# A selective-scan hybrid block: decays written into the state's tile, the scalar engine three states ahead, transfers issued one planner step later, and one row fetch per state in place of two

## The chip, the cores and the metric

The kernel runs on one core of one Trainium2 chip. A core has a matrix engine (PE, whose weight loads the profile shows as PEld), a vector engine (DVE), a scalar engine (ACT), GpSimd (POOL) and SyncE (SP), which here only issues transfers. Each engine works through its own list of instructions in order, and an instruction waits at the head of its list until the semaphores that it names have been reached. Transfers are carried out by 16 DMA engines that the core's queues share. The metric is the device time in microseconds (us) of the whole launch; a kernel's time is the median of its runs.

## The reference, cut to what matters

The input is a batch of 8 images of 64 x 64 pixels and 96 channels, in float32. Layer 0 is a group norm, an in-projection to 2 x 192 channels, a 3 x 3 depthwise convolution with SiLU, a selective scan along four directions (diagonals and anti-diagonals, each forward and backward), a layer norm, a gate and an out-projection. Layer 1 is a linear attention without softmax and a feed-forward part whose operands are rounded to 8-bit floats. The scan dominates the work:

```python
def step(hst, inp):
    u_t, d_t, B_t, C_t = inp
    hst = hst * jnp.exp(d_t[..., None] * A) + (d_t * u_t)[..., None] * B_t[:, :, None, :]
    return (hst, jnp.einsum('bkdn,bkn->bkd', hst, C_t))
h0 = jnp.zeros((Bsz, K, D_INNER, D_STATE), jnp.float32)
_, yL = jax.lax.scan(step, h0, (uL, dL, BL, CL))
ys = jnp.moveaxis(yL, 0, -1) + Dk[None, :, :, None] * xs
```

There are K = 4 directions, 192 inner channels, D_STATE = 16 states for each channel, and 4096 positions in an image. Each state is a recurrence of its own: a decay exp(d A), a feed (d u) B, the running value h, and a product with C that is summed over the 16 states.

## The kernel before

**Tiling.** Positions lie along the free dimension, 512 at a time (T). The partitions hold 64 channels of two directions at once (d = 0 and 1), and G = 3 groups make up the 192 channels; so one state of one chunk is a tile of 128 x 3 x 512. The order of chunks is `steps`: for each of 8 images (b), two passes (q = 0 forward, q = 1 backward) over 8 chunks (c), 128 steps in all. Each step goes through its 16 states, so that the main loop (L1155) has 2048 iterations, one state each. In what follows i is the iteration, m the step and n the state in it.

**One state.** ACT computes the decay (`decay`, L961): three ACTIVATEs with Exp, one for each group, into a tile of the tag "decay" with three buffers. The feed comes in one of three ways, by the letter of `FEED = "DADADAGADADAAAAA"` (L48). In an A state ACT multiplies the turned rows of d u with B (`times_b`, L968, L988), eight ACTIVATEs into feedT (two buffers), and PE turns these back into the three PSUM tiles feed[0..2] (`turn`, L996). In the one G state POOL does ACT's eight products (L979). In a D state PE broadcasts B into feed[0] (L998) and DVE multiplies it with d u (L1013). Then DVE runs the recurrence with one scan instruction for each group (`recur`, L1000, scan at L1009), from the decay tile and the feed into an h tile, which has six buffers. POOL keeps the last column for the next chunk (`keep`, L1025) and multiplies h in place with C (`read`, L1030). C comes as the tile cc of 128 x 512, whose two halves hold one row each, repeated over 64 partitions: `fetch` (L952) reads the two rows from a DRAM tile crow, with two transfers (L957); cc has five buffers. Last, PE adds the products up by transposing them into one PSUM tile y (`reduce`, L1032, L1044).

**The order of an iteration.** Iteration i issues the decay of state i + 2, some background work for ACT, `times_b` of i + 2, the scans of i, then for three parts the turn of i + 1 and the reduce of i - 4 (`LAG = 4`) with background work for PE between, the keep and read of i - 1, background work for POOL, and the fetch of i + 4. The program text sets each engine's order; the tile framework adds the waits. A tile of a tag with N buffers waits for the last users of the tile N before it.

**Background work.** All that is not a state is written as Python generators and spread by a planner, `Work` (L261): `measures` and `front` (norm, convolution, gate, and the walk along the diagonals) for the next image, `tail` (join, attention, feed-forward) for the image before, and `prologue` (L879), which makes d, d u, B and C of the step after next. A generator yields a request: an engine, a cost in us, perhaps a lag, and whether it needs one of two PSUM banks. The planner places it when the engine's credit for the iteration allows (`PLACES`) and no earlier than a lag that depends on the two engines (`LAGS`; after a transfer, three iterations). The requests of tag "S", for SP, are looked at when an iteration begins (`next`, L337). Where there is no scan work to lean on, `finish` and `hurry` run the background alone.

**Transfers.** All transfers are issued from SP's one queue, in program order: also a transfer whose data are not made yet waits at the head of that queue, and what was issued later waits behind it. In this kernel a transfer stands right behind the instruction that makes its data: gate at L561, seq at L599, mid at L689, turned at L728, out at L834, crow at L910, part at L1072 (an image's first pass) and wide at L1089 (the second). The table gives the sizes.

Of the kernel before, what the change touches and what calls it, by code (L numbers as in the profile page):

```python
# [255 lines left out]


SPIN = ("P", 0.0, -1, False)


class Work:  # L261
# [104 lines left out]
    def finish(self, enough):  # L366

        self.alone = True
        while not enough():
            self.next()  # L370
            for tag, place in (("A", 0), ("V", 0), ("P", 2), ("G", 0)):
                self.at(tag, place)
        self.alone = False
        self.credit = dict.fromkeys(self.PLACES, 0.0)

    def hurry(self, enough):

        self.alone = self.hurried = True
        while not enough():
            self.now += 1  # L380
            for tag, place in (("A", 0), ("V", 0), ("P", 2), ("G", 0)):
                self.at(tag, place)
        self.alone = self.hurried = False
# [90 lines left out]
def front(tc, work, x, k, at, b):  # L474
# [8 lines left out]
    with tc.tile_pool(name=f"f1_{b}", bufs=1, **area) as p1, tc.tile_pool(name=f"f2_{b}", bufs=2, **area) as p2:  # L483
# [33 lines left out]
        def convolve(c):  # L517
# [41 lines left out]
            nc.scalar.activation(z, z, AF.Silu)  # L559
            k.tables()  # L560
            nc.sync.dma_start(out=at.gate[:, :, c * CH : (c + 1) * CH], in_=z)  # L561

# [13 lines left out]
    with tc.tile_pool(name=f"f3_{b}", bufs=3, **area) as p2:  # L576

        def walk(c):
# [12 lines left out]
            for g in range(G):  # L591
# [4 lines left out]
                nc.scalar.copy(u[:, g, :], ps)  # L596
                work.release(ps)
            for d in range(2):
                nc.sync.dma_start(  # L599
                    out=at.seq[d][:, c * T : (c + 1) * T].rearrange("(g i) t -> i g t", i=GC),  # L600
                    in_=u[d * GC : (d + 1) * GC],
                )
# [5 lines left out]
def tail(tc, work, x, out, k, at, b, last=False):  # L608
# [4 lines left out]
    with tc.tile_pool(name=f"t1_{b}", bufs=1, **area) as p1:  # L613
# [5 lines left out]
        with tc.tile_pool(name=f"t2_{b}", bufs=8 if last else 2, **area) as p2:  # L619
# [3 lines left out]
            def join(c):  # L623
# [63 lines left out]
                nc.scalar.copy(t, po)  # L687
                if not last:
                    nc.sync.dma_start(out=at.mid[:, s, :], in_=t)  # L689
                work.release(ps)  # L690
# [34 lines left out]
                if last:  # L725
                    kept[c] = t, xaT
                else:
                    nc.sync.dma_start(out=at.turned[:, c * CH : (c + 1) * CH], in_=xaT)  # L728
                joined.add(c)
# [32 lines left out]
        with tc.tile_pool(name=f"t3_{b}", bufs=8 if last else 3, **area) as p2:  # L762

            def layers(c):
# [67 lines left out]
                nc.gpsimd.tensor_tensor(y16, y16, k.b2q, ALU.add)  # L832
                nc.gpsimd.tensor_tensor(t, t, y16, ALU.add)
                nc.sync.dma_start(out=out[b].rearrange("(t p) c -> p t c", p=P)[:, s, :], in_=t)  # L834

# [3 lines left out]
def run(tc, psum, dram, x, out, w, NB):  # L839
# [33 lines left out]

    made, decays, feeds, hs, carry, sums, other = {}, {}, {}, {}, {}, {}, {}
    feed = [psum.tile([P, T], F32, tag=f"feed{g}", name=f"feed{g}") for g in range(G)]
# [3 lines left out]
    def prologue(m):  # L879
# [27 lines left out]
        nc.scalar.activation(x, v, AF.Identity, bias=w.xb)  # L907
        work.release(ps)
        o.crow = dram.tile([2 * NS, T], F32, tag="crow", name=f"crow_{m}", bufs=3)
        nc.sync.dma_start(out=o.crow, in_=x[XC:NX, :])  # L910
# [3 lines left out]
        for g in range(G):  # L914
            ps = yield bank(0.85)
            nc.tensor.matmul(ps, w.ws[:, q, g, :], x[0 : 2 * NR + 1, :], start=True, stop=True)  # L916
# [35 lines left out]
    def fetch(i):  # L952

        m, n = divmod(i, NS)
        cc = made[m].c[n] = pool.tile([P, T], F32, tag="cc", name=f"cc_{i}", bufs=5)
        for d in range(2):
            nc.sync.dma_start(  # L957
                out=cc[d * GC : (d + 1) * GC], in_=made[m].crow[d * NS + n : d * NS + n + 1, :].to_broadcast([GC, T])
            )

    def decay(i):  # L961
        m, n = divmod(i, NS)
        _, q, _ = steps[m]
        decays[i] = pool.tile([P, G, T], F32, tag="decay", name=f"decay_{i}", bufs=3)
        for g in range(G):
            nc.scalar.activation(decays[i][:, g, :], made[m].delta[:, g, :], AF.Exp, scale=w.a_neg[:, q, g, n : n + 1])  # L966

    def times_b(i):  # L968
# [3 lines left out]
        if FEED[n] == "D":  # L972
            return
        f = feeds[i] = pool.tile([P, TB * G, P], F32, tag="feedT", name=f"feedT_{i}", bufs=2)
        if FEED[n] == "G":
# [24 lines left out]
    def recur(i):  # L1000
        m, n = divmod(i, NS)
        _, q, _ = steps[m]
        h = hs[i] = pool.tile([P, G, T], F32, tag="h", name=f"h_{i}", bufs=6)
        a = decays.pop(i)
        back = slice(None, None, -1) if q else slice(None)

        def scan(g):
            init = carry[m - 1][:, n, g : g + 1] if m % NST else 0.0
            nc.vector.tensor_tensor_scan(h[:, g, back], a[:, g, back], feed[g][:, back], init, ALU.mult, ALU.add)  # L1009

# [47 lines left out]
    def place(m):  # L1058
# [7 lines left out]
        for d in range(2):  # L1066
# [3 lines left out]
            )  # L1070
        if q == 0:
            nc.sync.dma_start(out=image(b).part[:, c, :], in_=ys)  # L1072
        else:
            work.start(spread(m, rows), urgent=True)

    def spread(m, rows):
        b, q, c = steps[m]
        for d in range(2):
            yield gp(1.8, 1)
            nc.gpsimd.tensor_tensor(  # L1080
                rows[:, d], rows[:, d], other[m].rearrange("p (d k c) -> p d k c", d=2, k=TB)[:, d], ALU.add
            )
            stride = (3 * WW + 1) * DI if d == 0 else (3 * WW - 1) * DI
            for v in range(2):
# [59 lines left out]

    LAG = 4
    for i in range(4):
        fetch(i)
    for i in range(2):
        decay(i)
# [5 lines left out]
    for i in range(total + LAG + 1):  # L1155
# [13 lines left out]
        work.next()  # L1169
        if i + 2 < total:  # L1170
            decay(i + 2)
        work.at("A")
        if i + 2 < total:
            times_b(i + 2)
        if i < total:
# [104 lines left out]
```

## Time and profile before

| what | value |
|---|---|
| three runs, us | 11243.42, 11231.5, 11244.23 |
| median, us | 11243.42 |
| the profiled execution's own time, us | 11245.66 |
| its span from first to last instruction, us | 11243.9 |
| granted clock of PE, mean over the span | 0.907 |
| cc transfers | 4096 of 128.0 KB, median issue 588 ns |
| decay ACTIVATE (L966), mean of one | 714 ns |
| feedT ACTIVATE (L988), mean of one | 445 ns |
| scan (L1009), mean of one, with carry / without | 1262 / 1201 ns |
| product with C (L1030), mean of one | 3457 ns |

The profile is of one execution. Busy time is the time in which an engine had an instruction at work; a busy PE is not PE at its peak, since matmuls are pipelined. A line of waits reads: who (engine, tile, line) waited for whom, the total in us, how many times, and the longest. SPq is SP's queue of transfers. The chain is followed back from the last instruction, at each step to what released it, so that it shows what set the end. "DMA share" is the mean busy share of the 16 DMA engines. The first cc transfer is issued at 224.4 us and the last at 10984.2 us: before and after lie the first image's front and the last image's tail.

### The profile page before, as it was taken

To read this page: it belongs to the slowest core of one execution; us is meant where nothing else is said; L and a number is where in the kernel's file an instruction comes from. 1 tells how busy PE (TensorE), PEld (TensorE's weight loads), DVE (VectorE), ACT (ScalarE), POOL (GpSimd) and SP (SyncE) were. 2 spreads that over 40 slices of the span, in tenths; PEclk is the share of its full clock that TensorE was granted. 3 is DMA by queue.
4 is the path that set the end of the run, shared out by engine and by line. 5 is a ranking of instruction groups with operands and counts; after the bars stand their busy time and mean duration, and the time that the engine had idled before them with its cause. 6 is when DMAs were issued, how large, how long until landed. Compare 5 with 4: busy or idle time off the path is not lost.

```text
span 11243.9 us, 182845 instructions
## 1 busy us (share of the span) xinstructions
PE 9140.0 (81%) x60885; PEld 7661.4 (68%) x60885; DVE 9396.9 (84%) x10582; ACT 9455.9 (84%) x19651; POOL 9365.4 (83%) x7047
## 2 busy tenths in 40 slices
PE   6888788878888788878888788887888878878884
PEld 5677677666676667766677666776667666666663
DVE  2988988888888888888888888888898888989993
ACT  3888888888888888888888888888898888888883
POOL 1877987899878998789987899779997799998994
PEclk8999999888998889988999898998999988889886
DMA  3335333543335443354334543345433543432332
GB/s 91 106 92 143 100 98 92 144 118 102 97 93 149 110 108 95 96 144 113 102 92 113 138 107 102 92 118 134 109 99 90 133 119 104 108 103 84 99 94 63
DMA packets 1122742, 1206.98 MB, mean 107 GB/s; under 512 B 452790, under 2 KB 730007, under 8 KB 1121799
## 3 DMA queue, kind: packets, MB, share of 16 engines
q1 hardware_dynamic: 1121798, 1195.28, 40.3%
q8 instruction: 485, 7.95, 0.3%
q14 instruction: 459, 3.75, 0.1%
HBM read 874.83 MB, written 319.98 MB: 106 GB/s over the span
## 4 chain that ended last, share of the span: by engine, by line
PE 24%; ACT 23%; DVE 17%; POOL 14%; issue 10%; DMA 7%; SPq 4%; DVEq 0%; POOLq 0%; ACTq 0%
DVE h L1009 11%; ACT feedT L988 9%; POOL h L1030 8%; ACT decay L966 7%; PE y L1044 7%; PE feed L996 7%; DMA cc<-crow 4%; DVE feed L1013 4%; PE bank L542 3%; SPq L587 2%; PE bank L894 2%; PE feed L998 1%; ACT L63 1%; POOL du L928 1%; DMA y<-wide 1%
## 5 line engine op out<-in xcount | busy, mean ns | idle before, releaser
L1030 POOL TENSOR_TENSOR h<-h,cc 128x1536 f32<-128x1536 f32 x2048 | 7079.9, 3457 | 458.3 <-DMA cc<-crow 228.9
L1009 DVE TENSOR_TENSOR_SCAN h<-decay,carry,feed 128x512 f32<-128x512 f32 x5376 | 6514.2, 1262 | 810.2 <-PE feed L996 704.8
L966 ACT ACTIVATE decay<-delta,a_neg 128x512 f32<-128x512 f32 x6144 | 3975.0, 714 | 1116.4 <-DVE h L1009 1114.4
L996 PE MATMUL feed<-ident,feedT 128*128 128x128 f32 x16896 | 3090.8, 303 | 1649.1 <-DVE h L1009 1084.6
L1044 PE MATMUL y<-ident,h 128*128 128x128 f32 x24576 | 3847.4, 290 | 130.7 <-POOL h L1030 47.4
L996 PEld LDWEIGHTS feed<-ident,feedT 128*128 128x128 f32 x16896 | 2209.1, 155 | 2246.9 <-ACT feedT L988 840.8
L988 ACT ACTIVATE feedT<-duT,rows 128x192 f32<-128x192 f32 x10240 | 3673.7, 445 | 17.6 <-PE feed L996 14.7
L1044 PEld LDWEIGHTS y<-ident,h 128*128 128x128 f32 x24576 | 3164.5, 152 | 525.2 <-issue 410.3
L1013 DVE TENSOR_TENSOR feed<-feed,du 128x512 f32<-128x512 f32 x1920 | 1200.4, 685 | 162.2 <-PE feed L998 146.5
L1025 POOL COPY carry<-h 128x3 f32<-128x3 f32 x2048 | 402.5, 197 | 877.0 <-DVE h L1009 803.2
L1009 DVE TENSOR_TENSOR_SCAN h<-decay,feed 128x512 f32<-128x512 f32 x768 | 879.5, 1201 | 118.9 <-PE feed L996 106.8
L542 PE MATMUL bank<-wf,xp 97*128 97x192 f32 x4266 | 851.9, 332 | 0.0
L998 PE MATMUL feed<-x,pick 77*128 77x512 f32 x1280 | 708.8, 636 | 3.9
L542 PEld LDWEIGHTS bank<-wf,xp 97*128 97x128 f32 x4266 | 692.8, 194 | 5.4 <-issue 4.6
L928 POOL TENSOR_TENSOR du<-delta,u 128x1536 f32<-128x1536 f32 x128 | 448.4, 3503 | 188.8 <-ACT delta L921 188.8
L916 PE MATMUL bank<-x,ws 13*128 13x512 f32 x764 | 435.5, 650 | 5.6 <-ACT x L907 5.6
L979 POOL TENSOR_TENSOR feedT<-duT,rows 128x512 f32<-128x512 f32 x384 | 396.2, 1060 | 4.7 <-PE feed L996 4.7
L894 PE MATMUL bank<-wx,u 128*128 128x77 f32 x3048 | 360.0, 275 | 0.0
L894 PEld LDWEIGHTS bank<-wx,u 128*128 128x128 f32 x3048 | 352.3, 193 | 1.9 <-ACT duT L936 0.2
L918 DVE COPY delta<-bank 128x512 f32<-128x512 f32 x382 | 256.7, 672 | 86.5 <-PE bank L916 86.1
L934 PE MATMUL bank<-ident,du 128*128 128x128 f32 x1532 | 251.8, 291 | 65.1 <-POOL du L928 61.8
L998 PEld LDWEIGHTS feed<-x,pick 77*128 77x128 f32 x1280 | 211.5, 200 | 97.6 <-DVE h L1009 44.8
(261 smaller groups left out, 6957.4 us busy)
## 6 DMA issues: line engine op xcount, KB each, us to landing
cc<-crow SPq DMA_DIRECT2D x4096, 128.0 KB
u<-seq SPq DMA_DIRECT2D x256, 384.0 KB
wide<-ys SPq DMA_DIRECT2D x512, 192.0 KB
ut<-image SPq DMA_DIRECT2D x768, 64.0 KB
seq<-us SPq DMA_DIRECT2D x128, 384.0 KB
part<-ys SPq DMA_DIRECT2D x64, 768.0 KB
y<-part SPq DMA_DIRECT2D x64, 768.0 KB
y<-wide SPq DMA_DIRECT2D x256, 192.0 KB
```

The source lines that it names most:

```text
L542: nc.tensor.matmul(v[:, j, :], flat[:, o : o + P], k.wf[:, i, :], start=(i == 0), stop=(i == 8), skip_group_check=True)
L894: nc.tensor.matmul(v[:, j, :], u[:, g, j * P : (j + 1) * P], w.wx[:, q, g, :], start=(g == 0), stop=(g == G - 1))
L916: nc.tensor.matmul(ps, w.ws[:, q, g, :], x[0 : 2 * NR + 1, :], start=True, stop=True)
L928: nc.gpsimd.tensor_tensor(du, delta, u, ALU.mult)
L966: nc.scalar.activation(decays[i][:, g, :], made[m].delta[:, g, :], AF.Exp, scale=w.a_neg[:, q, g, n : n + 1])
L988: nc.scalar.activation(f[part], o.duT[part], AF.Copy, scale=o.rows[:, j, XB + d * NS + n : XB + d * NS + n + 1])
L996: nc.tensor.transpose(feed[g][:, j * P : (j + 1) * P], feeds[i][:, j * G + g, :], w.ident)
L998: nc.tensor.matmul(feed[0], w.pick[:, FEED[:n].count("D"), :], made[m].x, start=True, stop=True)
L1009: nc.vector.tensor_tensor_scan(h[:, g, back], a[:, g, back], feed[g][:, back], init, ALU.mult, ALU.add)
L1013: nc.vector.tensor_tensor(feed[g], feed[0], made[m].du[:, g, :], ALU.mult)
L1030: nc.gpsimd.tensor_tensor(hs[i], hs[i], c.unsqueeze(1).to_broadcast([P, G, T]), ALU.mult)
L1044: nc.tensor.matmul(y[:, j, :], hs[i][:, g, r * P : (r + 1) * P], w.ident, is_transpose=True, start=(n == 0 and j % 4 == 0), stop=(n == NS ...
```

## The change

Four things are changed.

1. The decay of a state is written into the state's own h tile, and the scan overwrites it in place. The tag "decay" goes, and h has eight buffers in place of six.
2. ACT works three states ahead (`AHEAD = 3`) in place of two, for the decays and for `times_b`; feedT has three buffers in place of two.
3. A new request, `LATER`, of tag "S" and lag 1, stands in front of the transfers of gate, seq, out, crow, part and wide, and of mid and turned together, which are moved to one place. The generator goes on at the start of the next iteration or later, so that the transfer stands that much later in SP's order. The store of part becomes a small generator, `first_rows`. `finish` and `hurry` look at "S" as well. The first bank request in prologue after crow is given a lag of 0.
4. `fetch` reads both rows of a state with one transfer of 128 x 512 in place of two of 64 x 512.

```diff
@@ -255,6 +255,7 @@
     return "P", us, lag, "long" if long else "short"
 
 
+LATER = ("S", 0.0, 1, False)
 SPIN = ("P", 0.0, -1, False)
 
 
@@ -368,7 +369,7 @@
         self.alone = True
         while not enough():
             self.next()
-            for tag, place in (("A", 0), ("V", 0), ("P", 2), ("G", 0)):
+            for tag, place in (("A", 0), ("V", 0), ("P", 2), ("G", 0), ("S", 0)):
                 self.at(tag, place)
         self.alone = False
         self.credit = dict.fromkeys(self.PLACES, 0.0)
@@ -378,7 +379,7 @@
         self.alone = self.hurried = True
         while not enough():
             self.now += 1
-            for tag, place in (("A", 0), ("V", 0), ("P", 2), ("G", 0)):
+            for tag, place in (("S", 0), ("A", 0), ("V", 0), ("P", 2), ("G", 0)):
                 self.at(tag, place)
         self.alone = self.hurried = False
 
@@ -558,6 +559,7 @@
             nc.scalar.activation(pre[:, 0 : len(tiles), :], pre[:, 0 : len(tiles), :], AF.Silu)
             nc.scalar.activation(z, z, AF.Silu)
             k.tables()
+            yield LATER
             nc.sync.dma_start(out=at.gate[:, :, c * CH : (c + 1) * CH], in_=z)
 
             image = at.image[0 : HH * DOUBLE].rearrange("(h a x c) -> h x a c", a=2, c=DI, x=WW)
@@ -595,6 +597,7 @@
                 yield act(0.6)
                 nc.scalar.copy(u[:, g, :], ps)
                 work.release(ps)
+            yield LATER
             for d in range(2):
                 nc.sync.dma_start(
                     out=at.seq[d][:, c * T : (c + 1) * T].rearrange("(g i) t -> i g t", i=GC),
@@ -685,8 +688,6 @@
                         )
                 yield act(0.5)
                 nc.scalar.copy(t, po)
-                if not last:
-                    nc.sync.dma_start(out=at.mid[:, s, :], in_=t)
                 work.release(ps)
                 yield dve(1.7)
                 for i in range(4):
@@ -725,6 +726,8 @@
                 if last:
                     kept[c] = t, xaT
                 else:
+                    yield LATER
+                    nc.sync.dma_start(out=at.mid[:, s, :], in_=t)
                     nc.sync.dma_start(out=at.turned[:, c * CH : (c + 1) * CH], in_=xaT)
                 joined.add(c)
 
@@ -831,6 +834,7 @@
                 yield gp(2.0)
                 nc.gpsimd.tensor_tensor(y16, y16, k.b2q, ALU.add)
                 nc.gpsimd.tensor_tensor(t, t, y16, ALU.add)
+                yield LATER
                 nc.sync.dma_start(out=out[b].rearrange("(t p) c -> p t c", p=P)[:, s, :], in_=t)
 
             yield [layers(c) for c in range(NCH)], 8 if last else 3
@@ -871,7 +875,7 @@
             )
         return images[b]
 
-    made, decays, feeds, hs, carry, sums, other = {}, {}, {}, {}, {}, {}, {}
+    made, feeds, hs, carry, sums, other = {}, {}, {}, {}, {}, {}
     feed = [psum.tile([P, T], F32, tag=f"feed{g}", name=f"feed{g}") for g in range(G)]
     banks = [psum.tile([P, T], F32, tag=f"bank{i}", name=f"bank{i}") for i in range(2)]
     work = Work(banks + feed)
@@ -906,13 +910,14 @@
         x = o.x = tile("x", [NX, T])
         nc.scalar.activation(x, v, AF.Identity, bias=w.xb)
         work.release(ps)
+        yield LATER
         o.crow = dram.tile([2 * NS, T], F32, tag="crow", name=f"crow_{m}", bufs=3)
         nc.sync.dma_start(out=o.crow, in_=x[XC:NX, :])
 
 
         delta = tile("delta", [P, G, T])
         for g in range(G):
-            ps = yield bank(0.85)
+            ps = yield bank(0.85, None if g else 0)
             nc.tensor.matmul(ps, w.ws[:, q, g, :], x[0 : 2 * NR + 1, :], start=True, stop=True)
             yield dve(0.6)
             nc.vector.tensor_copy(delta[:, g, :], ps)
@@ -953,17 +958,17 @@
 
         m, n = divmod(i, NS)
         cc = made[m].c[n] = pool.tile([P, T], F32, tag="cc", name=f"cc_{i}", bufs=5)
-        for d in range(2):
-            nc.sync.dma_start(
-                out=cc[d * GC : (d + 1) * GC], in_=made[m].crow[d * NS + n : d * NS + n + 1, :].to_broadcast([GC, T])
-            )
+        nc.sync.dma_start(
+            out=cc, in_=made[m].crow.rearrange("(d n) t -> d n t", n=NS)[:, n : n + 1, :].to_broadcast([2, GC, T])
+        )
 
     def decay(i):
+
         m, n = divmod(i, NS)
         _, q, _ = steps[m]
-        decays[i] = pool.tile([P, G, T], F32, tag="decay", name=f"decay_{i}", bufs=3)
+        hs[i] = pool.tile([P, G, T], F32, tag="h", name=f"h_{i}", bufs=8)
         for g in range(G):
-            nc.scalar.activation(decays[i][:, g, :], made[m].delta[:, g, :], AF.Exp, scale=w.a_neg[:, q, g, n : n + 1])
+            nc.scalar.activation(hs[i][:, g, :], made[m].delta[:, g, :], AF.Exp, scale=w.a_neg[:, q, g, n : n + 1])
 
     def times_b(i):
 
@@ -971,7 +976,7 @@
         o = made[m]
         if FEED[n] == "D":
             return
-        f = feeds[i] = pool.tile([P, TB * G, P], F32, tag="feedT", name=f"feedT_{i}", bufs=2)
+        f = feeds[i] = pool.tile([P, TB * G, P], F32, tag="feedT", name=f"feedT_{i}", bufs=3)
         if FEED[n] == "G":
             d = 2
             scale = o.rows[:, :, XB : XB + d * NS].rearrange("p j (d n) -> p j d n", d=d)[:, :, :, n]
@@ -1000,13 +1005,12 @@
     def recur(i):
         m, n = divmod(i, NS)
         _, q, _ = steps[m]
-        h = hs[i] = pool.tile([P, G, T], F32, tag="h", name=f"h_{i}", bufs=6)
-        a = decays.pop(i)
+        h = hs[i]
         back = slice(None, None, -1) if q else slice(None)
 
         def scan(g):
             init = carry[m - 1][:, n, g : g + 1] if m % NST else 0.0
-            nc.vector.tensor_tensor_scan(h[:, g, back], a[:, g, back], feed[g][:, back], init, ALU.mult, ALU.add)
+            nc.vector.tensor_tensor_scan(h[:, g, back], h[:, g, back], feed[g][:, back], init, ALU.mult, ALU.add)
 
         if FEED[n] == "D":
             for g in (1, 2, 0):
@@ -1068,10 +1072,12 @@
                 rows[:, d].rearrange("p k (g i) -> p k g i", i=GC),
                 y.rearrange("p (k g) (d i) -> p d k g i", g=G, d=2)[:, d],
             )
-        if q == 0:
-            nc.sync.dma_start(out=image(b).part[:, c, :], in_=ys)
-        else:
-            work.start(spread(m, rows), urgent=True)
+        work.start(spread(m, rows) if q else first_rows(m, ys), urgent=True)
+
+    def first_rows(m, ys):
+        b, _, c = steps[m]
+        yield LATER
+        nc.sync.dma_start(out=image(b).part[:, c, :], in_=ys)
 
     def spread(m, rows):
         b, q, c = steps[m]
@@ -1080,6 +1086,7 @@
             nc.gpsimd.tensor_tensor(
                 rows[:, d], rows[:, d], other[m].rearrange("p (d k c) -> p d k c", d=2, k=TB)[:, d], ALU.add
             )
+            yield LATER
             stride = (3 * WW + 1) * DI if d == 0 else (3 * WW - 1) * DI
             for v in range(2):
                 for again in range(2):
@@ -1142,10 +1149,10 @@
         work.now += tag == "A"
         work.at(tag, at)
 
-    LAG = 4
+    AHEAD, LAG = 3, 4
     for i in range(4):
         fetch(i)
-    for i in range(2):
+    for i in range(AHEAD):
         decay(i)
         times_b(i)
     for g in range(G):
@@ -1167,11 +1174,11 @@
             if n == NS // 2 and m + 2 < len(steps):
                 bring(m + 2)
         work.next()
-        if i + 2 < total:
-            decay(i + 2)
+        if i + AHEAD < total:
+            decay(i + AHEAD)
         work.at("A")
-        if i + 2 < total:
-            times_b(i + 2)
+        if i + AHEAD < total:
+            times_b(i + AHEAD)
         if i < total:
             recur(i)
         else:
```

## The prediction

> **What bounds the kernel now.** I read the page first, then who waited for whom, then SP's own waits, then the chain and single stretches around odd transfers.
>
> ```profile
> PE 9140.0 (81%) x60885; PEld 7661.4 (68%) x60885; DVE 9396.9 (84%) x10582; ACT 9455.9 (84%) x19651; POOL 9365.4 (83%) x7047
> ...
> q1 hardware_dynamic: 1121798, 1195.28, 40.3%
> ```
>
> Four engines are 81 to 84% busy: none is the bound alone, and what is lost is lost between them. The 16 DMA engines are 40.3% busy on average, which looks like room. The waits:
>
> ```profile
> ACT decay L966 <- DVE h L1009: 1114.4, 556, 7.3
> ...
> DVE h L1009 <- PE feed L996: 811.6, 729, 4.4
> ...
> PE feed L996 <- ACT feedT L988: 435.1, 757, 4.5
> ...
> POOL h L1030 <- DMA cc<-crow: 228.9, 34, 18.7
> ```
>
> ACT idles for DVE to give back a decay buffer, and elsewhere DVE idles for PE, which idles for ACT's turned rows: ACT is ahead by too little to carry the five A states in a row at the end of FEED. POOL waits for its rows cc only 34 times. SP's queue:
>
> ```profile
> SPq L957 <- POOL carry L1025: 1982.1, 682, 8.8
> SPq L957 <- POOL h L1030: 1410.5, 484, 7.2
> SPq L1072 <- ACT ys L1067: 399.2, 49, 12.1
> SPq L561 <- ACT z L559: 352.6, 64, 7.3
> ```
>
> SP mostly waits for POOL to free a cc buffer, which is only the ring's pacing. The others are transfers issued right behind the instruction that makes their data; the cc fetches queue behind them. Last, the lines that decide this case. The list of transfers has cc in pieces of 128 KB, and two kinds of 97 rows of 2 KB (194.0 KB: turned, stored at L728, and xaT, loaded at L774); the chain, with start and length, holds a turned store, and an issue of L776 that lasted 6.11 us:
>
> ```profile
> cc<-crow SPq DMA_DIRECT2D x4096, 128.0 KB
> ...
> xaT<-turned SPq DMA_DIRECT2D x56, 194.0 KB
> ```
>
> ```profile
> 2597.82 6.11 SPq L776
> ...
> 5000.42 10.22 DMA turned<-y
> ```
>
> The next view is single stretches: five engines' busy time with counts, PE clock, DMA share of 16, GB/s. In the first an xaT load (issued 2680.14) is draining almost alone; in the second an image piece of 34 positions (issued 1748.37); in the third one of 64 positions; the fourth is the span from the first cc to the last.
>
> ```profile
> 2686.00:2690.00 4.00, 4.00 (x27) 3.68 (x26) 2.01 (x3) 4.00 (x10) 3.92 (x3) 0.69 0.07 25
> 1749.20:1749.90 0.70, 0.34 (x3) 0.19 (x3) 0.00 (x0) 0.70 (x3) 0.70 (x1) 1.00 0.14 31
> 1750.00:1750.60 0.60, 0.60 (x7) 0.60 (x6) 0.45 (x1) 0.60 (x2) 0.60 (x1) 1.00 0.72 223
> 224.00:10985.00 10761.00, 8869.31 (x59443) 7446.02 (x59442) 9289.57 (x10245) 9315.97 (x19392) 9242.13 (x6749) 0.91 0.41 109
> ```
>
> One engine of 16 is a share of 0.0625. So 97 rows ran on one engine (0.07, 25 GB/s, and 10.22 us in the chain for 198,656 B), 34 on two (0.14), 64 on about all (0.72). 97 is prime; 34 is 2 x 17; 64 is 4 x 16. The rows look like a split over the largest count up to 16 that divides the outer dimension. And SP's 6.11 us inside one issue (L776, behind two L774 loads of xaT) show that a backlog on one engine holds SP's whole queue.
>
> **The change part by part.** Reckoned against the profiled execution: span 11,243.9, 11,245.66 with what lies around it, 2 us above the median 11,243.42 of the runs shown.
>
> *The merged cc transfer.* Before: two issues a state, each 64 rows of 2 KB, with 64 as outer dimension on both sides: all 16 engines. After: one issue, whose source counts 2 outermost (the directions), then 64 repeats of one row, and whose target counts 128 partitions. No row before has unlike counts on its two sides. The ends are therefore 16 engines (the target decides) and 2 (the source does). A cut must fall at the same places on both sides, and what suits 2 and 128 is 2: I take two engines, the case of the 34-position row. SP saves 2048 issues of 0.588 us (median of L957), 1,204 us, worth nothing by itself, since SP waits 3,393 us for POOL (1,982.1 + 1,410.5) anyway.
>
> On two engines each carries 64 rows a state, 131,072 B. At 25 GB/s that is 5.24 us, at 24 (the print also holds small packets) 5.46; I take 24.5: 5.35 us. The state's whole period is now 10,761 / 2048 = 5.25 us. So cc alone fills the two engines, and cover by the other work is gone. The busier engine carries besides:
> - the rest of the traffic: 1195.28 MB less 4096 x 128 KB (536.9) is 658.4 MB, 41.1 MB an engine. At 25 GB/s 1,646 us. From above: 40.3% of the span is 4,531 us an engine; less cc's old 33.6 MB at 25 GB/s (1,342) leaves 3,189. By bytes 2,496. With 14 engines emptier there is less jostling, so I take 2,070, halfway between 1,646 and 2,496.
> - the 112 single-engine transfers (turned, xaT), if they go to one of the two: 112 x 198,656 B at 24.5 is 908 us, less the 57 in the average: 850.
>
> Before the first cc and after the last lie 224 + 259 = 483 us, where other traffic took 0.37 and 0.27 of the engines, 153 us, which does not add. Sum: 10,957 (2048 x 5.35) + 2,070 + 850 - 153 + 483 = 14,207. To this I add 200 for stretches in which the engine is not fed, between nothing and 300, an estimate from the 229 us that POOL waits for cc now: about 14,400. Ends: 10,737 + 1,646 + 850 + 330 = 13,563; 11,185 + 3,189 + 850 + 330 + 300 = 15,854. Five cc buffers hide latency, not throughput: POOL is late next, then PE's reduce, then the h buffers, then ACT.
>
> The Trainium skill ("DMA: Bandwidth & Descriptors", section on why a DMA increments its semaphore by 16) says that a transfer takes the largest number of engines up to 16 that divides the slowest dimension above 1 of both sides; by it cc has the same two engines and the sum stands. The rows of 97, 34 and 64 agree; none here shows unlike sides. The same page's bandwidth section advises larger transfers for efficiency, which speaks for merging; by that alone this part would cost nothing and the total stay that of the rival below. The 97-row load, bigger than one cc and far slower, is the row against it.
>
> *Later transfers.* gate, seq, mid with turned, out, crow, part and wide go out one planner step after their data are made. The transfers themselves are the same; they move past at most one state's cc fetch, and readers come steps later. What can go is POOL's 228.9 us for cc; what can come is a late seq or part, of which no row shows more. 0 to -229 alone; under the two-engine queue nothing, as SP is held anyway. The 0 in prologue's bank request keeps it from inheriting a lag of 3.
>
> *Decays in h, three states ahead, three feedT.* No instruction is added: 6144 decay ACTIVATEs of 714 ns, 10,240 of 445, 6144 scans of about 1,255. The scan now reads and writes one tile; in-place L1013 (685 ns) stands near the plain copy L918 (672 ns), so I cost that at nothing. A wait is exchanged: decay(i+3) needs h of state i-5, released by PE's reduce of iteration i-1, which comes behind turn of state i and so behind the scan of i-1. The old wait was that scan itself, for a decay of i+2. ACT gains a state less about eight 128-wide PE operations. Queued behind this wait on ACT are times_b and the copies that free PE's two banks. The gain lies between nothing and DVE's 811.6 us; I take PE's 435.1 us for turned rows if cc keeps all engines, and nothing if cc is the bound. Space: 6 + 3 + 2 tiles of 6 KB become 8 + 3, the same. At the start one more decay, 2.1 us on ACT.
>
> **The rivals.**
> 1. *cc spread over 16 engines (the other side).* Place: the queue's split of L957. The target's 128 decides; the ACT lead then removes the 435.1: 11,246 - 435 = 10,811, from 10,435 (all 811.6) to 11,200. For it: the 64-row transfers. Against: the 97-row ones. The deciding point: eight engines would do, since a state's cc is then 1.34 us each.
> 2. *Spread, but the lead is given back.* The third state of lead is lost because PE waits for banks that a lagging ACT frees, or because decay now waits for reduce. For it: PE's place in both loops; against: ACT's own 1,114.4 us wait. 11,246 + 0 to 150: about 11,300.
> 3. *Two engines that run faster than the xaT load.* 64 reads of one row could be quicker. To be hidden, 131,072 B must fit into 5.25 us less other traffic of 2,070 / 2048 = 1.0 us: 31 GB/s an engine. The stretches above show 25, 15.5 a piece of the two, and 223 over 11.5 engines, 19: none reaches it. At 28 GB/s: 9,587 + 2,070 + 850 + 330 = 12,837.
>
> **How the numbers follow.** Two engines at the seen rate 0.87; rival 1 0.07; rival 2 0.03; rival 3 0.03. The bound for "same", 0.2%, is 22 us and about what a measurement can tell. Faster: rival 1, 0.07. Same: 0.02 of rival 2. Slower: 0.87 + 0.03 + 0.01 = 0.91. The range is the likeliest case's: 13,563 to 15,854, rounded outward to 13,450 and 15,900. It holds nine in ten of that case, so 0.78 in all; rivals 1 to 3 lie below it.
>
> **What would show it.** cc<-crow x2048 of 256.0 KB, with a median issue time of L957 far above 0.588 us. POOL's wait for cc in thousands of us and the chain's DMA cc<-crow from 4% to the largest share. All compute engines near 65%; the granted clock higher or equal. DMA share in the slices below 4 tenths although DMA is the bound, with stretches at 0.13 and 50 GB/s. Operation means unchanged (L1009, L966, L988); ACT's wait for DVE replaced by one for PE's reduce. I am wrong if single stretches show a cc transfer at a share near 1, or if cc's waits stay near 229 us; the time then is that of rivals 1 or 2.

## The result, and the profile after

| kernel | runs | median, us | lowest to highest, us |
|---|---|---|---|
| before | 4 | 11243.83 | 11231.5 to 11251.55 |
| changed | 4 | 14630.74 | 14628.57 to 14633.18 |

The changed kernel takes 1.3014 times as long, with a 95% interval of 1.2991 to 1.3036. The profiled execution's span is 14,626.8 us, with a mean granted PE clock of 0.814 (before 0.907). The page's first part and its line of the DMA queue:

```profile
PE 9799.2 (67%) x60885; PEld 8268.1 (57%) x60885; DVE 9455.3 (65%) x10582; ACT 9500.9 (65%) x19651; POOL 9306.3 (64%) x7047
...
q1 hardware_dynamic: 1060358, 1195.04, 27.7%
```

The four compute engines do as many instructions as before. DVE, ACT and POOL are busy for the same time within 1%, PE for 7% longer, at a lower clock (9,799 us against 9,140); the rest of the added time is waiting. The DMA engines moved the same 1,195 MB and look idler than before, 27.7% against 40.3%. That mean over 16 engines is what misleads. The view of who waited for whom (in us: total, times, longest), and all cc transfers (issue time in ns: least, median, most):

```profile
POOL h L1034 <- DMA cc<-crow: 4207.4, 1294, 27.1
DVE h L1013 <- PE feed L1001: 2729.2, 978, 21.5
ACT h L971 <- PE y L1048: 1546.6, 463, 28.3
```

```profile
L961 SPq DMA_DIRECT2D cc<-crow x2048: 487/3344/8991, 223.9 to 14358.6; - x187
```

POOL waits 4,207 us for cc in place of 229, in 1,294 states of 2,048. SP's median cc issue lasts 3.34 us in place of 0.588: SP itself is held. Single stretches show why. The columns are again five engines' busy time with counts, PE clock, DMA share, GB/s:

```profile
7006.00:7008.00 2.00, 0.00 (x0) 0.00 (x0) 0.09 (x1) 0.00 (x0) 0.00 (x0) 0.97 0.07 26
7010.00:7012.00 2.00, 2.00 (x10) 1.70 (x9) 0.00 (x0) 0.00 (x0) 0.00 (x0) 0.50 0.13 50
7016.00:7018.00 2.00, 2.00 (x21) 2.00 (x20) 2.00 (x2) 2.00 (x7) 0.00 (x0) 1.00 0.13 50
224.00:14359.00 14135.00, 9531.50 (x59499) 8056.36 (x59497) 9358.55 (x10254) 9368.45 (x19410) 9185.02 (x6749) 0.82 0.28 83
```

From 7010 on cc drains: a share of 0.13 is two engines of 16, and 50 GB/s is 25 for each. Two microseconds earlier an xaT load of 97 rows drains alone, on one engine (0.07, 26 GB/s), and hardly any compute engine works. The timeline of the same place (start, length, engine, line; idle time before and what ended it in brackets):

```profile
7000.51 7.42 SPq L779 DMA_DIRECT2D t<-mid  x1
7004.81 1.28 DVE L1013 TENSOR_TENSOR_SCAN h<-h,carry,feed 128x512 f32<-128x512 f32 x1 [19.66 <-PE feed L1001]
7008.04 16.59 SPq L961 DMA_DIRECT2D cc<-crow  x4
...
7009.05 1.65 PE L782 MATMUL bank<-t,ident 128*128 128x384 f32 x2 [3.91 <-DMA t<-mid]
...
7014.16 1.95 ACT L971 ACTIVATE h<-delta,a_neg 128x512 f32<-128x512 f32 x3 [26.57 <-PE y L1048]
...
7022.89 3.45 POOL L1034 TENSOR_TENSOR h<-h,cc 128x1536 f32<-128x1536 f32 x1 [26.97 <-DMA cc<-crow]
```

This is the chain of lateness in one place. SP sits 7.42 us in one issue, then 16.59 us over four cc issues; POOL gets its rows after 27 us; PE waits for a load of the background; and ACT, DVE, POOL wait 20 to 27 us each. From 7,006 to 7,008 the compute engines are idle together while one DMA engine streams, and POOL is idle throughout. Counted over the trace's packet records (packets of 64 B and more) from the first cc issue to the last, there are only 67 of 14,135 us in which no data packet was in flight; before, 3,617 of 10,760. In 9,187 us exactly two packets were in flight; before, in 264.

### The profile page after: what moved, and what is told of

It reads as the page before. It is cut to its first block, busy times and chain, and to the rows that moved or that the text cites. A ratio compares the mean times of both kernels' runs of the same rounds, so it can differ in the third digit from the quotient of the medians.

```text
span 14626.8 us, 179116 instructions
## 1 busy us (share of the span) xinstructions
PE 9799.2 (67%) x60885; PEld 8268.1 (57%) x60885; DVE 9455.3 (65%) x10582; ACT 9500.9 (65%) x19651; POOL 9306.3 (64%) x7047
## 3 DMA queue, kind: packets, MB, share of 16 engines
q1 hardware_dynamic: 1060358, 1195.04, 27.7%
## 5 line engine op out<-in xcount | busy, mean ns | idle before, releaser
L1013 DVE TENSOR_TENSOR_SCAN h<-h,carry,feed 128x512 f32<-128x512 f32 x5376 | 6549.0, 1264 | 2732.5 <-PE feed L1001 2520.9
L971 ACT ACTIVATE h<-delta,a_neg 128x512 f32<-128x512 f32 x6144 | 3973.1, 712 | 3126.2 <-PE y L1048 1546.6
L1048 PE MATMUL y<-ident,h 128*128 128x128 f32 x24576 | 4089.5, 303 | 429.1 <-POOL h L1034 421.4
L1048 PEld LDWEIGHTS y<-ident,h 128*128 128x128 f32 x24576 | 3371.9, 160 | 912.9 <-POOL h L1034 532.6
L1001 PEld LDWEIGHTS feed<-ident,feedT 128*128 128x128 f32 x16896 | 2356.6, 164 | 1857.2 <-DVE h L1013 941.7
L1013 DVE TENSOR_TENSOR_SCAN h<-h,feed 128x512 f32<-128x512 f32 x768 | 881.7, 1201 | 230.6 <-PE feed L1001 208.3
L939 PEld LDWEIGHTS bank<-ident,du 128*128 128x128 f32 x1532 | 202.0, 161 | 995.4 <-POOL du L933 929.7
L941 ACT COPY duT<-bank 128x512 f32<-128x512 f32 x383 | 217.6, 568 | 647.4 <-PE bank L939 647.4
L898 PE MATMUL bank<-wx,u 128*128 128x77 f32 x3048 | 452.7, 316 | 201.1 <-DMA u<-seq 198.6
L596 PE MATMUL bank<-ident,ut 128*128 128x128 f32 x748 | 147.6, 333 | 472.2 <-DMA ut<-image 459.9
```

The source lines that it names most:

```text
L898: nc.tensor.matmul(v[:, j, :], u[:, g, j * P : (j + 1) * P], w.wx[:, q, g, :], start=(g == 0), stop=(g == G - 1))
L939: nc.tensor.transpose(ps[:, i * P : (i + 1) * P], du[:, g, r * P : (r + 1) * P], w.ident)
L971: nc.scalar.activation(hs[i][:, g, :], made[m].delta[:, g, :], AF.Exp, scale=w.a_neg[:, q, g, n : n + 1])
L1001: nc.tensor.transpose(feed[g][:, j * P : (j + 1) * P], feeds[i][:, j * G + g, :], w.ident)
L1013: nc.vector.tensor_tensor_scan(h[:, g, back], h[:, g, back], feed[g][:, back], init, ALU.mult, ALU.add)
L1048: nc.tensor.matmul(y[:, j, :], hs[i][:, g, r * P : (r + 1) * P], w.ident, is_transpose=True, start=(n == 0 and j % 4 == 0), stop=(n == NS ...
```

## The experiments

Ratios are to runs of the kernel before on the same chip; in brackets the 95% interval.

| kernel | median, us | ratio |
|---|---|---|
| before, with the one merged fetch alone | 14640.83 | 1.3024 (1.2998 to 1.3050) |
| changed, two fetches again | 11179.69 | 0.9948 (0.9931 to 0.9964) |
| changed, merged fetch in half of the states | 11558.64 | 1.0282 (1.0262 to 1.0303) |
| changed, merged fetch in three quarters | 12552.97 | 1.1167 (1.1145 to 1.1189) |
| changed, merged fetch from four rows | 11384.93 | 1.0120 (1.0100 to 1.0140) |
| before, later transfers alone | 11249.62 | 1.0000 (0.9990 to 1.0009) |
| before, decays in h and three ahead alone | 11185.79 | 0.9943 (0.9928 to 0.9957) |
| two fetches, two states ahead | 11144.49 | 0.9909 (0.9892 to 0.9925) |
| two fetches, background first | 11018.25 | 0.9791 (0.9775 to 0.9807) |
| before, background first | 11389.48 | 1.0121 (1.0106 to 1.0137) |
| two fetches, 97 rows cut into 96 and 1 | 11165.58 | 0.9921 (0.9906 to 0.9936) |
| two fetches, background first, rows cut | 10994.59 | 0.9775 (0.9760 to 0.9789) |

**Does the merged fetch carry the whole loss?** It was put into the kernel before alone:

```diff
-        for d in range(2):
-            nc.sync.dma_start(
-                out=cc[d * GC : (d + 1) * GC], in_=made[m].crow[d * NS + n : d * NS + n + 1, :].to_broadcast([GC, T])
-            )
+        nc.sync.dma_start(
+            out=cc, in_=made[m].crow.rearrange("(d n) t -> d n t", n=NS)[:, n : n + 1, :].to_broadcast([2, GC, T])
+        )
```

> The kernel before with the one merged fetch and nothing else. Two-engine theory (cc runs on two of 16 DMA engines, the busier one is the bound): the whole loss is here, 14,400 to 14,900 us, with single stretches of cc at a DMA share near 0.13. Rival (part of the loss is due to later transfers, or to the decays in h waiting for reduce): clearly less, under 14,000 us.

It took 14,640.83 us, 10 us from the changed kernel. The chain of this kernel reaches from end to end (that of the changed kernel covers only its last 500 us). First the chain's lines of the kernel before, then this kernel's by engine and by line:

```profile
DVE h L1009 11%; ACT feedT L988 9%; POOL h L1030 8%; ACT decay L966 7%; PE y L1044 7%; PE feed L996 7%; DMA cc<-crow 4%; DVE feed L1013 4%; PE bank L542 3%; SPq L587 2%; PE bank L894 2%; PE feed L998 1%; ACT L63 1%; POOL du L928 1%; DMA y<-wide 1%
```

```profile
DMA 49%; POOL 16%; PE 11%; SPq 9%; ACT 7%; DVE 5%; issue 3%; POOLq 0%; DVEq 0%; ACTq 0%
DMA cc<-crow 39%; POOL h L1029 10%; DVE h L1008 3%; PE feed L995 3%; ACT feedT L987 3%; PE y L1043 3%; DMA u<-seq 2%; ACT decay L965 2%; DMA gate<-z 2%; POOL du L928 2%; DMA image<-pre 2%; SPq L956 1%; SPq L587 1%; SPq L776 1%; PE bank L542 1%
```

The transfer of cc, 4% of the chain before, is 39% now. The loss is this edit's, and the other three edits change nothing that can be told beside it.

**What is the rest of the change worth?** The two fetches were put back in the changed kernel (the same diff the other way).

> The changed kernel with the two 64-row fetches put back. Two-engine theory: all of the loss goes, and the rest of the change shows what it is worth: 10,435 to 11,300 us, 10,800 if PE's wait for ACT's turned rows goes as reckoned. Rival (the rest carries part of the loss): over 11,300 us.

It took 11,179.69 us: 0.5% less than before, inside the range but at its weak end. Its waits:

```profile
DVE h L1014 <- PE feed L1002: 514.6, 489, 7.2
ACT h L972 <- PE y L1049: 502.7, 252, 7.8
...
PEld feed L1002 <- ACT feedT L994: 288.0, 194, 4.3
...
PEld bank L939 <- ACT duT L941: 191.6, 124, 3.0
...
PE bank L939 <- ACT duT L941: 162.3, 121, 2.8
POOL h L1035 <- DMA cc<-crow: 156.8, 35, 17.6
...
PE feed L1002 <- ACT feedT L994: 115.6, 115, 4.0
```

DVE's wait for PE fell by 297 us (811.6 to 514.6), but the span by 64 only. A new wait stands in the list that the kernel before did not have: PE waits for ACT to empty a bank (duT).

**Throughput or a price for each transfer?** The merged fetch was used in half and in three quarters of the states:

```diff
+        if n % 2:
             nc.sync.dma_start(
                 out=cc, in_=made[m].crow.rearrange("(d n) t -> d n t", n=NS)[:, n : n + 1, :].to_broadcast([2, GC, T])
             )
+        else:
+            for d in range(2):
+                nc.sync.dma_start(
+                    out=cc[d * GC : (d + 1) * GC], in_=made[m].crow[d * NS + n : d * NS + n + 1, :].to_broadcast([GC, T])
+                )
```

> The changed kernel with the merged fetch in odd states only, two 64-row fetches in the even ones. Throughput theory: the busier engine has 1024 x 5.35 + 1024 x 0.67 us of cc and 2,920 of other traffic, about 9,080 us, less than the 10,761 us of the loop before: mostly hidden, within 400 us of the kernel with two fetches throughout. Rival (each merged transfer costs a wait of its own, whatever the engine's total): half of the loss, some 12,700 us.

> The merged fetch in three states of four. Throughput theory: 1536 x 5.35 + 512 x 0.67 + 2,920 + 330 us is 11,810, with the 3% that the changed kernel lay above its sum 12,160: 11,800 to 12,400 us. Rival (a wait for each merged transfer): three quarters of the loss, some 13,700 us.

The second has `n % 4` in place of `n % 2`. Measured: 11,558.64 and 12,552.97 us. Over the kernel with two fetches these are +379, +1,373, and +3,451 for all states: the first half of the transfers costs 379 us and the second 3,072. A price for each transfer would have given 1,726 and 2,588. So it is throughput, with a soft knee: the half lies just within the 400 us expected, three quarters 153 us above its range. POOL's wait for cc in the two:

```profile
POOL h L1040 <- DMA cc<-crow: 575.7, 105, 25.0
```

```profile
POOL h L1040 <- DMA cc<-crow: 2121.7, 654, 27.5
```

The packet records say the same: from the first cc issue to the last, 65 of 12,062 us are without a data packet with three quarters merged, as few as with all, and 876 of 11,060 with half (3,560 of 10,694 with two fetches throughout). Why the knee is soft is argued, not shown: transfers may bunch, since with half of the states merged the sum for the engine fits into the loop, yet POOL waited up to 25 us and at 105 places.

**Is it the number 2?** In this kernel crow holds each of its rows twice, and the one merged fetch reads four rows of a state, each repeated 32 times. Each step stores crow with four transfers in place of one.

```diff
-        o.crow = dram.tile([2 * NS, T], F32, tag="crow", name=f"crow_{m}", bufs=3)
-        nc.sync.dma_start(out=o.crow, in_=x[XC:NX, :])
+        o.crow = dram.tile([4 * NS, T], F32, tag="crow", name=f"crow_{m}", bufs=3)
+        for r in range(4):
+            first = XC + r // 2 * NS
+            nc.sync.dma_start(out=o.crow[r * NS : (r + 1) * NS], in_=x[first : first + NS, :])
...
-            out=cc, in_=made[m].crow.rearrange("(d n) t -> d n t", n=NS)[:, n : n + 1, :].to_broadcast([2, GC, T])
+            out=cc, in_=made[m].crow.rearrange("(r n) t -> r n t", n=NS)[:, n : n + 1, :].to_broadcast([4, P // 4, T])
```

> The changed kernel with its one merged fetch, but crow holds each of its rows twice, so that the source counts 4 outermost and 32 repeats; the target still counts 128. Theory (the split follows the largest common divisor up to 16, here 4): 32 rows of 2 KB an engine and state, 2.68 us, 5,480 us in all and about 8,400 with the other traffic, less than the loop's 10,761; mostly hidden, 11,180 to 11,560 us, with stretches of cc at a DMA share near 0.25. Rival (a transfer with unlike outer counts is slow whatever they are): 14,000 us or more.

It took 11,384.93 us. Same bytes for a cc tile, same single issue, same target; the source's outer count went from 2 to 4, crow's store from one transfer to four, and the time fell from 14,631 us. A stretch in which cc drains, and the issue times:

```profile
7008.00:7009.40 1.40, 1.40 (x16) 1.40 (x14) 1.40 (x3) 1.40 (x6) 1.40 (x2) 1.00 0.26 102
```

```profile
L963 SPq DMA_DIRECT2D cc<-crow x2048: 507/524/4293, 225.4 to 11127.5; - x187
```

A share of 0.26 is four engines, 102 GB/s is 25.5 for each: in this stretch the rate of an engine is nearly that with two and with one. In 3,816 of the 10,902 us from the first cc issue to the last exactly four data packets were in flight. SP's median issue is down to 0.52 us. The kernel is still 205 us slower than the one with two fetches, and how much of that is the four engines' and how much the added stores' was not separated. A merged fetch with 16 or 64 outermost was not tried.

**Later transfers alone**: the kernel before with LATER in front of the moved transfers, and nothing else of the change.

```diff
+            yield LATER
             nc.sync.dma_start(out=at.gate[:, :, c * CH : (c + 1) * CH], in_=z)
```

> The kernel before with the later transfers alone (two fetches, decays in their own tile, two states ahead). Theory A (the 60 us that the changed kernel gains with two fetches come from ACT's lead): within 22 us of before. Theory B (they come from SP's queue, whose fetches no longer stand behind unfinished data): 11,180 us or less, with POOL's wait for cc well under 229 us.

11,249.62 us against 11,248.41, over ten runs: no change. POOL's wait for cc was 140.4 us in the profiled execution, in place of 228.9, and the time did not follow it:

```profile
POOL h L1036 <- DMA cc<-crow: 140.4, 36, 16.7
```

**Decays in h, three states ahead, three feedT alone**: the kernel before with the edits to `decay`, `recur`, feedT's buffers and the main loop.

```diff
-        decays[i] = pool.tile([P, G, T], F32, tag="decay", name=f"decay_{i}", bufs=3)
+        hs[i] = pool.tile([P, G, T], F32, tag="h", name=f"h_{i}", bufs=8)
...
-    LAG = 4
+    AHEAD, LAG = 3, 4
```

> The kernel before with decays in h, three states ahead and three feedT, two fetches, transfers where they were. Theory A (the gain is ACT's lead): about 11,180 us. Theory B (SP's queue): 11,220 to 11,260 us. In both PE's wait for ACT's turned rows falls from 435 us to about 116, and ACT's wait for DVE's scan gives way to one for PE's reduce.

11,185.79 us, the same as all of the change with two fetches. So the 60 us are of this edit. Its waits show the exchange that the prediction described, and the new one:

```profile
ACT h L966 <- PE y L1043: 681.0, 357, 8.5
...
PEld bank L934 <- ACT duT L936: 174.3, 115, 2.9
```

**Is it the third state of lead?** Here the changed kernel with two fetches has `AHEAD, LAG = 2, 4`; the eight h tiles, the scan in place and the third feedT stay.

> The changed kernel with two fetches, and ACT two states ahead again: the larger h ring, the scan in place and the third feedT stay. Theory (the 60 us come from the third state of lead): 11,220 to 11,260 us. Rival (they come from the buffers, which release ACT from DVE's scan): about 11,180 us.

11,144.49 us: below both. Two ahead is faster than three by some 0.4%, with intervals that just don't touch. My theory falls: the gain is that of what stayed, the larger ring with the scan in place and the third feedT, which no run takes apart. Its waits:

```profile
PEld feed L1002 <- ACT feedT L994: 763.7, 803, 5.0
...
PE feed L1002 <- ACT feedT L994: 319.5, 562, 3.3
...
ACT h L972 <- PE y L1049: 29.7, 29, 2.8
```

PE waits 319.5 us for turned rows here and 115.6 at three ahead, and yet this kernel is the faster one: that wait alone does not set the time. ACT goes down its own list as far as buffers let it; AHEAD only decides behind how many states' decays its background work stands. With the new ring the old wait of ACT for DVE's scan (1,114 us) is gone at either setting. At three, ACT waits 502.7 us for PE's reduce in place of 29.7, and PE 162.3 us for duT, a wait that is not in the list at two: the copies that free PE's banks come later.

**Where the gain is given back.** If it is that order, the background can go first in the iteration:

```diff
+        work.at("A")
         if i + AHEAD < total:
             decay(i + AHEAD)
-        work.at("A")
```

> The changed kernel with two fetches, where ACT's background work of an iteration stands ahead of the decay in place of behind it. Theory (the lead's gain is given back because PE waits for ACT to empty the two banks): PE's wait of 192 us for ACT's duT copies falls by half or more and the time falls by 50 to 200 us, to 10,980 to 11,130. Rival (the gain is lost elsewhere, as in the wait for PE's reduce before a decay): within 22 us of 11,180, or slower where decays now come late.

11,018.25 us, 161 less (177 by the two ratios, each to its own runs of the kernel before). PE's wait for duT fell by more than half, ACT's wait for reduce by half, and DVE's for PE once more:

```profile
DVE h L1014 <- PE feed L1002: 405.4, 452, 7.5
...
ACT h L972 <- PE y L1049: 243.2, 161, 3.1
...
ACT duT L941 <- PE bank L939: 102.8, 56, 8.3
...
PEld bank L939 <- ACT duT L941: 88.3, 70, 2.7
```

The control is the same order in the kernel before, with its small rings:

> The kernel before with nothing but ACT's background work of an iteration ahead of the decay. Theory (the order pays only where ACT is three states ahead, since there the banks are emptied late): within 100 us of before, 11,150 to 11,350, on either side. Rival (the order is worth 160 us by itself): 11,090 us or less.

11,389.48 us, 1.2% slower, and 39 us beyond the range. There ACT's turned rows come later still, and ACT stands waiting for PE:

```profile
PEld feed L996 <- ACT feedT L988: 1241.9, 1567, 4.3
```

```profile
ACT duT L936 <- PE bank L934: 273.2, 142, 8.3
```

So the order pays with the larger rings and three ahead, and costs without them; the larger rings with two ahead and the background first were not run. What is shown is that the place of the background work in ACT's list moves the time by 161 us with large rings. That the bank handover alone is the mechanism is argued from the waits: they moved in the same step as ACT's wait for reduce, and no run separates the two.

**The transfers of 97 rows.** In the kernel with two fetches turned and xaT were cut into 96 rows and 1:

```diff
-                        nc.sync.dma_start(out=xaT, in_=at.turned[:, c * CH : (c + 1) * CH])
+                    for r in (slice(0, DM), slice(DM, DM + 1)):
+                        nc.sync.dma_start(out=xaT[r], in_=at.turned[r, c * CH : (c + 1) * CH])
```

> The changed kernel with two fetches, and the transfers of 97 rows (turned and xaT) cut into 96 rows and 1. If one slow DMA engine is what holds SP and cc there, POOL's wait for cc falls from 157 us to under 60, no issue lasts over 3 us behind an xaT load, and the time falls by 50 to 150 us, to 11,030 to 11,130. Rival (the single-engine transfers are hidden by the cc buffers and by the planner's lags): within 22 us of 11,180.

The issue of t<-mid, which comes behind xaT, first in the kernel with whole rows and then in this one (ns: least, median, most):

```profile
L779 SPq DMA_DIRECT2D t<-mid x56: 332/703/9567, 2575.5 to 10362.8; - x56
```

```profile
L781 SPq DMA_DIRECT2D t<-mid x56: 332/338/407, 2584.4 to 10336.0; - x56
```

The mechanism is right: no issue of this load lasts over 0.41 us where one lasted 9.57. The worth is not: 11,165.58 us, 14 less, with intervals that overlap, and POOL's wait for cc fell from 156.8 to 115.9 us only, where under 60 was expected. It was hidden. With the better order:

> The changed kernel with two fetches, ACT's background work ahead of the decay, and the 97-row transfers cut into 96 rows and 1. If the two gains add: 11,018 less 15, about 11,000 us. If the cut is hidden once the banks are emptied early: 11,018 within 22 us.

10,994.59 us, 0.9775 of the time before (0.9760 to 0.9789): the fastest kernel of this study. The cut's own part, 24 us, is not told apart from nothing: the intervals with and without it overlap.

## Why the prediction was right, point by point

- **Two engines.** Right. The stretch at 0.13 and 50 GB/s is the one named beforehand, and the run with four rows shows that the source's outer count sets the split: four rows, four engines. No row of the trace before had unlike counts; the step from rows of equal counts to this one was an inference, and it held.
- **The rate of an engine**, taken as 24.5 GB/s from an xaT load, was a little high. In the packet records, stretches of thirty or more rows of 2 KB with two packets in flight (161,170 rows in all) give 85.3 ns a row on an engine, 24.0 GB/s. Single views print up to 25.
- **The sum.** 14,207 and 200 for stretches not fed, against 14,631. No packet at all was in flight for 67 us, which is the least that the busier engine can have stood unfed. If it is all, the 200 was too much and the other terms were 357 us too small together. Some 220 of these are cc's: 131,072 rows at 85.3 ns are 11,180 us in place of 10,957. What is left, 130 to 140 us, would then be the rest of the traffic, 2,200 in place of 2,070; this last step is a remainder and not a measurement. That the total came within 2% is in part luck: two misses of opposite sign.
- **The other edits cost and gain nothing where cc is the bound.** Right: 14,641 without them, 14,631 with them. The scan in place took 1,264 ns against 1,262.
- **Rival 1's price was wrong.** With the fetch on all engines it gave 10,811 and measured 11,180. The step that failed is that PE's whole 435 us wait for turned rows goes and comes back as time. That wait did go (115.6 us are left), but PE's for banks came (162 us by its matmuls, 192 by its weight loads), and ACT's for reduce, 503 us. Nor was the wait worth its length: with two ahead 319.5 us of it stay, and the time is 35 us shorter. Rival 2 named this mechanism, though it priced it at no gain or a loss. Both stood at 0.07 and 0.03 and are not told apart by their outcome: the measured 0.9948 lies between them.
- **Later transfers**, 0 to -229 us alone: 0.
- **The signs.** cc x2048 of 256 KB, the long issue, POOL's wait, the even 64 to 67% of the engines, and the exchange of ACT's wait all came as named. One was wrong: I wrote that the granted clock would be higher or equal, and it fell from 0.907 to 0.814.

## What to carry to other kernels

Before two transfers are merged into one, look at the outermost count of both sides: here 2 against 128 put a quarter of a megabyte on two of 16 DMA engines, and 4 against 128 on four; the two transfers of 64 against 64 were the fastest of the three. A mean DMA share of 28% can be a DMA bound; look at short stretches and compare the share with 1/16, 2/16, 4/16. And if a tile ring is lengthened so that an engine may run ahead, look at once at what stands behind the extra work in that engine's own list: here the order of the background work was worth 161 us, and a third state of lead without it cost some 35 us.

## What the runs showed of the hardware that was not expected

- **The PE clock fell with the waiting.** With the same matmuls the mean granted clock is 0.908 with two fetches, 0.898 with four rows, 0.891 with half merged, 0.860 with three quarters, and 0.813 with the merged fetch alone. The mean transpose of L1048 took 303 ns in place of 290 (L1044 before). Around the timeline above the clock changes at 7,004.46, 7,007.87 and 7,014.70 us, in steps of 3.41 us or twice that:

```profile
7004.46:7007.87 3.41, 0.68 (x6) 0.44 (x4) 1.28 (x1) 0.00 (x0) 0.00 (x0) 1.00 0.07 25
7007.87:7011.29 3.42, 2.24 (x6) 1.64 (x7) 0.00 (x0) 0.00 (x0) 0.00 (x0) 0.50 0.30 90
7011.29:7014.70 3.41, 3.41 (x17) 3.41 (x17) 1.28 (x1) 0.54 (x1) 0.00 (x0) 0.50 0.13 51
7014.70:7018.11 3.41, 3.41 (x33) 3.41 (x32) 2.32 (x2) 3.41 (x9) 0.00 (x0) 1.00 0.13 45
```

- The Trainium skill ("TensorE: Matmul & The Clock Gate", part 1 on the clock gate) says that the clock falls to half after a window of about 3.4 us without work and is restored after as long a busy one. The steps of 3.41 us, the fall to 0.50 and the full clock after the one stretch that PE filled agree with it. The fall itself came otherwise here: the stretch before it held 0.68 us of matmuls, and the clock fell 2.7 us after the last of them. Of the 617 falls in this profile, 138 followed a stretch of 3.41 us with no matmul on record; over all of them PE was busy for 23% of that stretch in the median. By these runs a window need not be empty.
- **A backlog on one or two DMA engines holds SP's queue**, not only its own transfers: 16.59 us over four cc issues, and 9.57 us inside an unrelated issue behind an xaT load. The same issue takes 0.34 us in the median, and 0.41 at most, once the 97 rows are cut.
- **The rate of one engine is nearly a constant** for rows of 2 KB: by the packet records, in stretches of thirty or more such rows, 25.0 GB/s where one engine drains and 24.0 where two do (changed kernel), 23.5 where four do (four rows).
